# One table of keys in place of a planner: the order of all engines in a two-layer graph attention kernel

## The chip, the cores and the metric

The kernel runs on one core of a Trainium2 chip. The metric is the device time of one execution in microseconds; the median of the runs is compared. The core has five instruction streams that matter here: TensorE (PE in the profile, with its weight loads as PEld), VectorE (DVE), ScalarE (ACT), GpSimd (POOL) and SyncE (SP), which here only starts transfers. [...]

## The reference

The input is a batch of 128 graphs of 128 nodes with 512 features, and a 128x128 adjacency matrix with weights for each graph. Two layers of attention with 8 heads of 64 follow each other; everything is float32. Cut to what matters:

```
# layer 0
Q, K, V = x @ W_q + b_q, x @ W_k + b_k, x @ W_v + b_v        # split into 8 heads
scores  = Q K^T / 8 + a_i + c_j + b_g + log(adj + 1e-9)      # a = x @ w_g[:512], c = x @ w_g[512:]
x       = softmax(scores) V + x
# layer 1
q, k, v = x @ Wq.T + bq, x @ Wk.T + bk, x @ Wv.T + bv
logits  = q k^T / 8 + log(clip(adj, 1e-8))
out     = (softmax(logits) v) @ Wo.T + bo
result  = layer_norm(x + out) * gamma + beta
```

## The kernel before

**Tiling.** The graphs are taken in groups of four (`G = 4`), so each layer has 32 groups (`NG`), and the loop of `fast_path` runs over t = 0 to 63: layer 0 for t < 32, layer 1 from t = 32. A group is 512 rows of x, held transposed in `XT[t]`. Every projection is a 512x512 by 512x512 product, done by Strassen's scheme with seven products P1 to P7. Five of them (P1 to P5) are split once more by the same scheme (`inner`: seven pairs of matmuls 128 columns wide), and P6 and P7 are plain (`product`: four pairs of 256 columns each). Every matmul is issued as two halves of 64 rows of the stationary operand. In groups 0 and 32 all seven are plain. The sums of inputs that Strassen needs are made on POOL (`outer_sums`, `inner_sums`, buffers `T`, `innerB`, `innerT`, `inner3`); sums of products are made by ACT copies and DVE additions in and out of four PSUM banks `bankA` (two of them), `bankB` and `bankC` (`matrix`, buffers `t1`, `u2`, `u3`, `s5`). Layer 0 has three such matrices per group (v, q, k), layer 1 four (v, q, k and the output matrix of the group before, `o_matrix`).

**Attention.** `score` does the 32 pairs of small matmuls of two graphs into the PSUM tiles `s_0` and `s_1`, then for each graph one exp on ACT, and one DVE product with the adjacency, the result of which is called E in the code and `h` or `xT` in the profile (it lies in those buffers). So no logarithm is taken and the softmax is not shifted by its largest value. `mix` multiplies E by V with a column of ones for the sums; DVE divides. If a sum leaves a safe range, a slower general path, which is not part of this case, would be taken. In layer 0 the gates `a` and `c` of a graph come from two POOL products with rows of `w_g` and two ACT activations that add up along the row (`gates`, buffer `gw`, eight pairs per group); exp needs `c`. Results of layer 0 are written to DRAM twice, in natural order (`x1d_n`) and in 32x32 blocks (`x1d_b`), which layer 1 loads transposed. In layer 1 the mixed rows go through DRAM as blocks (`x1d_o`) and come back into `gw`, as input of the output matrix; the layer-1 input is added by an accumulating transfer on POOL's queue (`residual`), and ACT, DVE and POOL do the layer norm (`norm_and_store`).

**Order of the work.** The code above issues nothing. The class `Plan` stands in for the engines: `record` notes each instruction with the ones that it must follow (`preds`, from what they read and write), and TensorE work is noted in units (`unit`), with a place in the nominal order and a cost. `mark` notes where each group t begins. At the end `issue` emits all noted instructions in one sequence, and each engine gets its own in that order, so every instruction of the profile has the line L585. The sequence is made by `schedule`: a list scheduler with costs for each kind of instruction (`cost`, `wait`, `run`), forward and backward by turns, with random stirring; the best turn by its own reckoning is taken. Then `periodic` replaces the keys of the middle groups by a table: `PATTERNS` has one row for groups 1 to 31 and one for groups 34 to 62, each with a period and a key for every instruction of a group, so that every group there has the same order relative to the group before. The rest (groups 0, 32, 33, 63 and what follows) keeps the order of the list scheduler, and `refine` then goes through the whole sequence twice and moves single instructions where TensorE would wait by its reckoning.

**Change of layers.** In group 32 the four weights of layer 1 are loaded and combined on POOL (`combine_outer`, `combine_inner`, buffers `w` and `wi`), while the gates and mixes of group 31 and the first layer-1 products also need POOL, DVE and PE. **The end** is written out after the loop: the last group's output is done graph by graph with plain matmuls, and the layer norms of groups 62 and 63 are spread over DVE, ACT and POOL, each followed by its store.

Of the kernel before, what the change touches and what calls it, by code (L numbers as in the profile page):

```python
# [13 lines left out]
ALU = mybir.AluOpType  # L14
# [29 lines left out]
class Strassen:  # L44
# [45 lines left out]
    def inner_weight(t, x, i):  # L90
# [10 lines left out]

PATTERNS = (
    (1, 31, 42.01, [int(v) for v in '''
        413 877 68 1327 2833 345 136 0 481 1462 1395 1039 549 2070 3356 809 626 694 1573 2772 8615 4503 9355 9402
        10016 10549 6965 8662 3435 3628 3876 4166 2912 3559 5020 4772 4414 5116 5731 6384 4000 4731 5185 5690 8495
        8668 8247 9001 8812 9064 9081 9671 10254 10385 9751 9898 10465 10663 10006 10137 10742 4665 4713 4779 4921
        5005 5071 5142 5225 5273 5318 5448 5514 5557 5645 5750 4975 5055 5121 5148 5186 5252 5295 5378 5426 5471
        5964 6095 6204 6248 6523 5612 5708 5774 5801 6008 6074 6139 6258 6299 6343 6430 6504 6570 6604 6685 6751
        6860 6956 7013 7142 7213 6621 6816 6882 6909 6947 7121 7268 7352 7399 7501 6548 6663 6682 6781 8688 6321
        6672 6772 6889 7958 9627 9517 10863 9873 9172 7034 7674 8061 7269 7382 8476 8659 8950 9298 9432 7596 7777  # L110
        8279 9364 10130 10643 10753 10261 10371 10596 9875 13411 13500 6357 6414 6520 6587 6641 6707 6772 6868 6991
        7035 7081 7312 7356 7465 7509 7575 7638 6398 6461 6649 6676 6728 6847 6903 7100 7246 7291 7733 7777 7886
        7930 8008 8053 7370 7421 7488 7514 7552 7623 7689 7755 7820 7865 7980 8061 8127 8154 8192 8258 8301 8367
        8432 8477 8598 8099 8148 8215 8241 8389 8455 8613 8679 8753 8798 7611 7842 7908 7935 7973 8040 8105 8180
        8279 8324 8370 8569 8657 8775 8819 8898 8944 7952 8017 8171 8198 8236 8302 8345 8411 8454 8538 9014 9057
        9123 9167 9414 9460 8641 8710 8776 8803 8863 8929 8970 9036 9101 9145 9232 9304 9370 9397 9435 9501 9544
        9610 9697 9742 9812 9505 9588 9654 9734 9807 9934 10257 10323 10388 10484 9957 10448 10609 10210 10344
    '''.split()]),
    (34, 62, 52.97, [int(v) for v in '''
        756 2204 2814 0 1409 1736 47 3975 4224 5312 4734 3324 4472 4995 5064 5133 5243 5984 5482 3282 3934 5441 5202  # L120
        4181 4329 4420 4001 4228 4247 4712 4869 4492 4602 4537 4954 5120 4771 4898 5585 5728 5871 5077 5432 5519
        6320 6100 5943 6210 13343 12372 16647 4432 4493 4559 4872 5033 5099 5345 5411 5563 5608 5678 5722 5831 5875
        5953 4588 4858 4937 5055 5213 5388 5476 5646 5765 5810 6093 6181 6268 6378 6444 5897 5962 6028 6055 6137
        6203 6334 6400 6465 6509 5925 6006 6072 6099 6225 6291 6421 6487 6531 6575 6646 6503 6552 6619 6646 6815
        6891 6946 7012 7077 7121 5658 5787 5854 5880 5918 5985 6050 6116 6312 6356 6402 6487 6596 6684 6727 6881
        6927 6582 6640 6746 6773 6858 6925 6990 7182 7252 7296 7099 7165 7208 7318 7471 7559 6718 6771 6837 6864
        6902 6968 7033 7100 7143 7203 7276 7361 7427 7454 7492 7571 7624 7690 7733 7785 7907 7652 7755 7821 7848
        7951 8029 8126 8193 8345 8389 7194 7274 7340 7367 7405 7480 7536 7602 7667 7712 7757 7820 7864 7908 7995
        8061 8107 7384 7449 7515 7542 7580 7646 7689 7755 7798 7846 8170 8258 8367 8454 8520 8566 7919 8039 8143
        8170 8214 8280 8411 8477 8542 8586 7979 8083 8226 8253 8301 8367 8498 8564 8605 8650 8720 8612 8671 8880  # L130
        8941 9058 9124 9189 9444 9572 9656 8802 9212 9325 9037 9150 5250 6137 6006 6701 8050 7967 8198 8327 7481
        8758 8129 8511 8888 8690 8998 9962 10155 10224 7316 8956 8456 9066 8462 8627 8693 8720 8758 8825 9014 9080
        9276 9465 9594 9637 9681 9725 9874 8659 8715 8897 8924 9145 9269 9435 9605 9768 9813 10046 10112 10199 10243
        10314 8795 9102 9168 9195 9233 9299 9391 9635 10090 10134 10207 10287 10414 10441 10554 10621 10686 10752
        10817 10965 11036 10387 10467 10533 10560 10598 10664 10729 10795 10839 10883 10961 12127 12252 12065 12243
        12272 12287 12304 12392 12414 12489 12654 12892 12967 13096 13227 11121 12654 12860 12716 13074 13244 13094
        13275 13794 14034 14405 15135 14120 14694 14942 15416
    '''.split()]),
)


class Plan:
# [5 lines left out]

    ENGINES = ("tensor", "vector", "scalar", "gpsimd", "sync")
    HOP, JUDGED, MARGINS = 0.06, 0.06, (0.05, 0.1, 0.15, 0.2)  # L150
    SAME = dict(tensor=0.0, vector=0.1, scalar=0.1, gpsimd=0.05, sync=0.0)
    DONE = dict(tensor=0.19, vector=0.085, scalar=0.085, gpsimd=0.04, sync=0.0)
    SEEN = dict(tensor=0.055, vector=0.035, scalar=0.035, gpsimd=0.09, sync=0.03)
    PATIENCE, PASSES, STIR = 40.0, 12, 0.6
    GRAIN, LATE, ROUGH, TRIALS = 32, 0.8, 0.8, 3
    AHEAD, STALL, SWEEPS, CALM = 400, 0.1, 2, 2.0

    class Op:
        __slots__ = ("i", "engine", "calls", "cost", "lag", "pos", "preds", "succs", "kb", "start", "ls")
# [8 lines left out]
    def __init__(self, tc):  # L168
        self.tc, self.nc = tc, tc.nc
        self.ops, self.seen, self.masks, self.open, self.log, self.marks = [], {}, {}, None, [], []  # L170
        self.patterns, self.fixed = (), 0
        for name in self.ENGINES:
            setattr(self, name, Plan.Engine(self, name))
# [4 lines left out]
    @contextmanager  # L178
    def unit(self, pos, cost):
        self.open = self.op("tensor", cost, pos=pos)  # L180
        yield
        self.open = None

    def op(self, engine, cost, lag=0.0, pos=None):
        o = Plan.Op()
        o.i, o.engine, o.calls, o.cost, o.lag, o.pos = len(self.ops), engine, [], cost, lag, pos
        o.preds, o.succs = set(), []
        self.ops.append(o)
        return o

    def record(self, engine, method, args, kw):
        aps = [(k, a) for k, a in list(enumerate(args)) + list(kw.items()) if hasattr(a, "tensor")]
        if engine == "tensor":
            o = self.open
        else:
            o = self.op(engine, *self.cost(engine, method, [a for _, a in aps], kw, args))
        o.calls.append((engine, method, args, kw))
        for k, a in aps:
            if k not in (0, "accum_out"):
                self.touch(o, a, False)  # L200
        for k, a in aps:
            if k in (0, "accum_out"):
                self.touch(o, a, True)

    @staticmethod
    def cost(engine, method, aps, kw, args):
        n = max(a.free_size() if callable(a.free_size) else a.free_size for a in aps)
        psum = any(a.space == PSUM for a in aps)
        if method == "dma_start":
            if engine == "gpsimd":  # L210
                return 1.6, 6.5
            kb = (aps[0].size() if callable(aps[0].size) else aps[0].size) * 4 / 1024
            return (1.1 if kb == 128 else 0.68) if len(aps[0].shape) == 4 else 0.47, 1.8 + kb / 150
        if engine == "scalar":
            return (0.06 + 0.00085 * n + (0.08 if "scale" in kw or "bias" in kw else 0.0) + (0.13 if "accum_out" in kw else 0.0),)
        if engine == "vector":
            if method in ("transpose", "bn_stats"):
                return (0.01 + 0.00118 * n,)
            if not psum and method in ("tensor_tensor", "tensor_scalar_mul") and n == 512:
                return (1.2,)  # L220
            return (0.08 + 0.00103 * n + (0.055 if method == "scalar_tensor_tensor" else 0.0),)
        if ALU.pow in args:
            return (0.68,)
        return (0.135 + 0.00216 * n,)
# [59 lines left out]
    def wait(self, p, o):  # L284

        if p.lag:
            return p.lag + self.HOP
        if p.engine == o.engine:
            return self.SAME[p.engine]
        return self.DONE[p.engine] + self.SEEN[o.engine]  # L290

    def run(self, edges, key):

        ops, start = self.ops, [0.0] * len(self.ops)
        free, left, when = dict.fromkeys(self.ENGINES, 0.0), [0] * len(ops), [0.0] * len(ops)
# [1113 lines left out]
```

## Time and profile before

| | |
|---|---|
| runs | 3132.68, 3135.54, 3135.10 us; median 3135.1 |
| profiled execution | 3135.12 us, span 3133.3 us, mean TensorE clock 0.995 |
| PE | busy 3079.3 us, 98% of the span |
| PE weight loads | 2667.8 us, 85% |
| DVE | 2262.5 us, 72% |
| POOL | 2233.0 us, 71% |
| ACT | 1796.7 us, 57% |
| DMA | mean 109 GB/s, 341.89 MB |
| PE in 400 to 800 us (layer 0) | busy 398.35 of 400 us |
| PE in 2000 to 2400 us (layer 1) | busy 398.53 of 400 us |
| PE in 0 to 80 us | busy 71.33 us |
| PE in 1300 to 1600 us | busy 284.88 us |
| PE in 3060 to 3134 us | busy 53.26 us |

The span is the time from the first to the last instruction of the core; the profiled execution's own time is 1.8 us longer. The profile's page gives totals, slices of the span, the chain of work that ended last and the costliest groups of instructions. The trace can be asked for single stretches (windows), for what an engine waited for (waits), and for single instructions in order of time (timeline); there, square brackets show how long the engine had been idle before the instruction, and what ended that. [...]

### The profile page before, as it was taken

What the parts mean: (1) busy time and instruction counts of PE and PEld (TensorE: products, weight loads), DVE (VectorE), ACT (ScalarE), POOL (GpSimd) and SP (SyncE); (2) the same over time, 40 slices, a digit from 0 to 9 for tenths busy, and PEclk for the clock granted to TensorE, in tenths of its full rate; (3) what the DMA queues carried; (4) which work ended last, traced back from release to release, by engine and by line L of the source; (5) the groups of instructions that cost most, each with busy time, mean ns of one, the idle gap of its engine ahead of it and who ended that gap; (6) DMA issues with size and microseconds to landing.
All of it is one profiled execution on the core that took longest, in us unless ns stands there. A gap on an engine that the chain in (4) does not pass through costs nothing.

```text
span 3133.3 us, 121185 instructions
## 1 busy us (share of the span) xinstructions
PE 3079.3 (98%) x50394; PEld 2667.8 (85%) x50394; DVE 2262.5 (72%) x5075; ACT 1796.7 (57%) x5179; POOL 2233.0 (71%) x2713
## 2 busy tenths in 40 slices
PE   8999999999999999989999999999999999999997
PEld 6888888888888888867888888888888888888885
DVE  5677777777677767765677777777777777777776
ACT  2666666666666665644565655565655555555653
POOL 8766666676666676688677786868686868686775
PEclk9999999999999999999999999999999999999999
DMA  5555555555555555553444444443435353535343
GB/s 116 115 106 115 108 112 123 117 108 113 110 110 122 123 110 108 123 140 76 107 102 111 105 106 110 102 114 93 118 91 123 89 127 84 129 83 130 86 110 92
DMA packets 963100, 341.89 MB, mean 109 GB/s; under 512 B 864240, under 2 KB 871408, under 8 KB 962544
## 3 DMA queue, kind: packets, MB, share of 16 engines
q1 hardware_dynamic: 944272, 299.48, 40.7%
q0 software_dynamic: 16864, 32.51, 6.3%
q8 instruction: 397, 6.50, 0.8%
q10 hardware_dynamic: 1408, 2.10, 0.2%
q14 instruction: 159, 1.30, 0.1%
HBM read 192.42 MB, written 141.56 MB: 107 GB/s over the span
## 4 chain that ended last, share of the span: by engine, by line
PE 88%; POOL 4%; DVE 2%; ACT 2%; issue 2%; DMA 1%; SPq 0%; ACTq 0%; DVEq 0%; POOLq 0%
PE bankA L585 42%; PE bankB L585 16%; PE bankC L585 15%; PE s L585 15%; POOL gw L585 2%; ACT s L585 1%; DVE kT L585 1%; POOL w L585 1%; ACT gw L585 1%; DMA xT<-in_x_dram 1%; POOL T L585 1%; POOL wi L585 0%; SPq L585 0%; DVE bankB L585 0%; POOL inner L585 0%
## 5 line engine op out<-in xcount | busy, mean ns | idle before, releaser
L585 PE MATMUL bankA<-T,w 128*64 128x256 f32 (+1 forms) x4232 | 519.8, 351 | 1.1 <-ACT bankA L585 0.8
L585 DVE TENSOR_TENSOR bankA<-bankA,s 128x128 f32<-128x128 f32 x868 | 256.0, 295 | 209.1 <-PE bankA L585 178.5
L585 DVE TENSOR_TENSOR bankB<-bankB,s 128x128 f32<-128x128 f32 x650 | 193.0, 297 | 214.3 <-PE bankB L585 170.8
L585 PEld LDWEIGHTS bankA<-T,w 128*64 128x64 f32 x4232 | 276.3, 137 | 46.3 <-ACT bankA L585 1.0
L585 DVE TENSOR_TENSOR bankC<-bankC,s 128x128 f32<-128x128 f32 x652 | 192.4, 295 | 156.5 <-PE bankC L585 125.7
L585 ACT ACTIVATE bankA<-ident 128x256 f32<-128x256 f32 x434 | 167.5, 386 | 197.4 <-DVE kT L585 117.9
L585 PE MATMUL bankA<-w,T 128*64 128x256 f32 (+1 forms) x2116 | 271.2, 352 | 0.9 <-POOL w L585 0.9
L585 PE MATMUL s<-qT,kT 64*128 64x128 f32 x4096 | 263.1, 278 | 1.1 <-DVE kT L585 1.0
L585 ACT COPY s<-bankA 128x128 f32<-128x128 f32 x434 | 114.2, 263 | 258.1 <-PE bankA L585 253.6
L585 POOL TENSOR_TENSOR rs<-rs,minus_half 128x2 f32<-128x2 f32 (+1 forms) x66 | 47.6, 722 | 298.7 <-ACT rs L585 298.7
L585 PEld LDWEIGHTS s<-qT,kT 64*128 64x128 f32 x4096 | 238.6, 188 | 23.7 <-issue 19.1
L585 PE MATMUL bankC<-xT,w 128*64 128x128 f32 (+1 forms) x2296 | 228.2, 277 | 0.4 <-ACT bankC L585 0.4
L585 ACT ACTIVATE gw<-gw 128x512 f32<-128x512 f32 x256 | 159.7, 625 | 99.6 <-POOL gw L585 99.6
L585 POOL TENSOR_TENSOR gw<-xn,gw 128x512 f32<-128x512 f32 x128 | 163.3, 1277 | 55.6 <-ACT gw L585 48.3
L585 POOL TENSOR_TENSOR gw<-w,gw 128x512 f32<-128x512 f32 x128 | 164.9, 1290 | 48.2 <-ACT gw L585 46.2
L585 POOL TENSOR_TENSOR h<-h,gamma 128x512 f32<-128x512 f32 x121 | 154.7, 1280 | 36.7 <-ACT h L585 36.7
L585 POOL TENSOR_TENSOR innerB<-xT 128x256 f32<-128x256 f32 x62 | 45.8, 738 | 187.5 <-PE bankB L585 122.8
L585 ACT ACTIVATE bankC<-ident 128x256 f32<-128x256 f32 x326 | 126.7, 389 | 91.3 <-DVE kT L585 48.6
L585 DVE STREAM_TRANSPOSE xT<-xT 128x512 f32<-128x512 f32 x252 | 172.6, 695 | 8.4 <-DMA w<-in_x_dram 8.4
L585 ACT ACTIVATE bankB<-ident 128x256 f32<-128x256 f32 x325 | 124.3, 383 | 87.6 <-DVE qT L585 34.8
L585 POOL TENSOR_TENSOR T<-xT 128x512 f32<-128x512 f32 x96 | 122.9, 1280 | 66.6 <-DVE xT L585 66.5
L585 PE MATMUL bankA<-w,xn 128*64 128x256 f32 x1364 | 165.8, 352 | 0.1
(268 smaller groups left out, 10172.8 us busy)
## 6 DMA issues: line engine op xcount, KB each, us to landing
xT<-x1d_b SPq DMA_DIRECT2D x64, 512.0 KB, 6.0
xT<-in_x_dram SPq DMA_DIRECT2D x496, 64.0 KB, 3.2
x1d_o<-o SPq DMA_DIRECT2D x248, 128.0 KB, 4.7
gw<-x1d_o SPq DMA_DIRECT2D x62, 512.0 KB, 3.4
h<-x1d_n POOLq DMA_DIRECT2D x62, 512.0 KB, 6.9
out_dram<-h SPq DMA_DIRECT2D x60, 512.0 KB, 4.0
xn<-in_x_dram SPq DMA_DIRECT2D x32, 512.0 KB, 4.1
x1d_n<-w SPq DMA_DIRECT2D x32, 512.0 KB, 3.8
```

The lines of the kernel that those rows point to most:

```text
L585: self.tc.keep_in_program_order(getattr(getattr(self.nc, engine), method)(*args, **kw))
```

## The change

The planner inside `Plan` goes: `cost`, `wait`, `run`, `edges`, `retime`, `first_keys`, `advance`, `refine`, `periodic` and `schedule` are removed, with their constants. In their place `tabled` gives every instruction a key from a table, and the sequence is again made by taking, of the instructions whose predecessors have been taken, the one with the least key. `PATTERNS` has new keys for the middle groups (3 to 29 and 36 to 60, with a first start and a period each), and the new `REST` has a key for each instruction of what lies before, between and behind: `FIRST` (860 keys: the set-up and groups 0 to 2), `CHANGE` (1978 keys: groups 30 to 35) and `LAST` (1158 keys: groups 61 to 63 and the end). The keys are in hundredths. The cost that `mix` hands to `unit` is changed as well; `unit` no longer uses it. The recording of the instructions and the finding of predecessors stay, and so does everything in `fast_path` but that cost and the last two lines.

```diff
 PATTERNS = (
-    (1, 31, 42.01, [int(v) for v in '''
-        413 877 68 1327 2833 345 136 0 481 1462 1395 1039 549 2070 3356 809 626 694 1573 2772 8615 4503 9355 9402
...
+    (3, 29, 71.95, 41.905, [int(v) for v in '''
+        0 2091 1819 2159 3282 230 115 1491 1245 2355 2023 2457 1887 2274 3842 1559 2389 1423 1955 3593 6418 4033
...
-    (34, 62, 52.97, [int(v) for v in '''
-        756 2204 2814 0 1409 1736 47 3975 4224 5312 4734 3324 4472 4995 5064 5133 5243 5984 5482 3282 3934 5441 5202
...
+    (36, 60, 1503.84, 52.968, [int(v) for v in '''
+        0 1486 1548 492 2912 3531 445 3872 4580 5040 4709 3569 3679 4902 5164 5274 5526 5347 5868 4374 5233 5416
...
+FIRST = 0.00, [int(v) for v in '''
+        1538 7625 29872 1229 1777 0 0 47 47 141 141 188 94 94 914 470 517 0 410 484 510 584 460 534 560 645 423 235
...
+CHANGE = 18.03, [int(v) for v in '''
+        120210 118718 118536 119847 122871 119055 120492 118652 120764 121818 120877 120560 120278 119848 122129
...
+LAST = 2828.05, [int(v) for v in '''
+        0 765 957 47 2973 3592 4706 4539 4540 4968 4661 2591 3085 4830 4785 4831 5458 5519 6565 4829 5457 4969 5588
...
+REST = FIRST, CHANGE, LAST
...
-    def periodic(self, start):
...
-    def schedule(self):
...
+    def tabled(self):
+
+        ops, marks, key = self.ops, self.marks, []
+        for group in range(len(marks) + 1):
+            row = next((v for v in self.patterns if v[0] <= group - 1 <= v[1]), None)
+            if row is not None:
+                first, _, start, period, at = row
+                key += [start + period * (group - 1 - first) + v / 100 for v in at]
+            elif not group or any(v[1] == group - 2 for v in self.patterns):
+                start, at = self.rest[sum(v[1] < group for v in self.patterns)]
+                key += [start + v / 100 for v in at]
+        assert len(key) == len(ops)
         after, left = [[] for _ in ops], [len(o.preds) for o in ops]
         for o in ops:
             for q in o.preds:
                 after[q].append(o.i)
...
+        heap, turn = [(key[o.i], o.i) for o in ops if not o.preds], []
+        heapify(heap)
         while heap:
             i = heappop(heap)[1]
-            seq.append(i)
+            turn.append(ops[i])
             for j in after[i]:
                 left[j] -= 1
                 if not left[j]:
                     heappush(heap, (key[j], j))
-        return seq
...
+        return turn
 
     def issue(self):
-        for o in self.schedule():
+        for o in self.tabled():
             for engine, method, args, kw in o.calls:
...
-        with nc.unit(pos, 0.93):
+        with nc.unit(pos, 0.985):
...
-    nc.patterns = PATTERNS
+    nc.patterns, nc.rest = PATTERNS, REST
     nc.issue()
```

## The prediction

> **What bounds the kernel now.** I read the totals and the slices first, then the chain, then the windows by stage, then the waits and short pieces of the timeline. The totals:
>
> ```profile
> PE 3079.3 (98%) x50394; PEld 2667.8 (85%) x50394; DVE 2262.5 (72%) x5075; ACT 1796.7 (57%) x5179; POOL 2233.0 (71%) x2713
> PE 88%; POOL 4%; DVE 2%; ACT 2%; issue 2%; DMA 1%; SPq 0%; ACTq 0%; DVEq 0%; POOLq 0%
> ```
>
> TensorE (PE) sets the end: busy 98% of the span and 88% of the chain that ended last. So only time in which PE waits, or in which nothing runs on it, can be won. By busy time that is 3133.3 - 3079.3 = 54 us. The windows (from:to, length, busy us and count of PE, its weight loads, DVE, ACT, POOL, then clock, DMA share, GB/s) say where:
>
> ```profile
> 0.00:80.00 80.00, 71.33 (x820) 52.78 (x822) 46.17 (x75) 25.02 (x65) 63.95 (x110) 0.96 0.54 114
> 400.00:800.00 400.00, 398.35 (x6670) 345.12 (x6670) 286.28 (x652) 247.29 (x731) 260.00 (x287) 1.00 0.55 115
> 1300.00:1600.00 300.00, 284.88 (x4447) 237.62 (x4442) 197.35 (x429) 148.85 (x416) 230.13 (x312) 0.99 0.43 107
> 2000.00:2400.00 400.00, 398.53 (x6638) 352.78 (x6634) 302.44 (x684) 232.22 (x657) 304.81 (x376) 1.00 0.42 102
> 3060.00:3134.00 74.00, 53.26 (x662) 38.84 (x656) 44.89 (x94) 25.15 (x71) 38.16 (x47) 0.89 0.31 87
> ```
>
> The middle of either layer shows 1.5 us idle in 400; start, change of layers and end show 8.7, 15.1 and 20.7. But busy time hides short waits. In the trace consecutive pairs of half matmuls start 218 ns apart (128 columns), 432 ns (256 columns), 116.5 ns (mix) or 112 ns (score) when nothing waits; a pair whose wait clears late is merely recorded as longer (0.44 us for 4 in place of 0.39 below). So I summed start-to-start times. One matrix is 5x7 pairs at 0.218 plus 8 at 0.432 = 11.09 us. A group of layer 0 has three matrices, two scores (4.18) and four mixes (3.73): 41.2 us. Layer 1 has a fourth matrix: 52.3. The chain gives the measured group, from one piece and the same piece 27 groups later (start, length, what):
>
> ```profile
> 158.24 1.99 PE s L585 x32
> 1306.49 1.99 PE s L585 x32
> 1580.06 2.16 PE bankA L585 x24
> 3011.78 2.16 PE bankA L585 x24
> ```
>
> (1306.49-158.24)/27 = 42.53 and (3011.78-1580.06)/27 = 53.03 us: 1.3 us of waiting per group in layer 0, 0.7 in layer 1. By the same sums the excess over unstalled matmuls is 12.1 us in 0-80, 2.4 in 80-150, 42 in 150-1300, 28.5 in 1300-1600, 25 in 1600-3000 and 6 after it up to the last matmul (3114.4), with 18.9 us behind that matmul. Some 5.5 us in each middle are inside the scores and no order removes them.
>
> [...]
>
> **The change part by part.** Comparing the two kernels' issue orders, every engine issues the same number of instructions (25360 PE, 5130 DVE, 4957 ACT, 2725 POOL, 1581 SP by that count); nothing but order differs, and the waits that follow from it. Nothing is saved by work removed; the mix's changed unit cost is not read any more. All gains are waits.
>
> *Layer 1, middle (36-60).* The repeated wait is this one:
>
> ```profile
> 1640.06 0.39 PE L585 MATMUL bankC<-inner,w 128*64 128x128 f32 x4
> 1640.28 0.30 DVE L585 TENSOR_TENSOR bankB<-bankB,s 128x128 f32<-128x128 f32 x1 [0.57 <-PE bankB L585]
> 1640.63 0.44 PE L585 MATMUL bankB<-innerT,w 128*64 128x128 f32 x4 [0.18 <-DVE bankB L585]
> ```
>
> Between the matmul that releases bankB to DVE and bankB's next use PE has one pair (0.218) to do, and the 0.30 operation with its signals takes longer. About 0.35 us are lost per group. In the new order no DVE-released bank has under about 297 ns of slack by my sum (before -77), and places with at most 450 ns fall from 16 to 6 per two groups. I take 0.35 x 25 groups = 8.8 us. Below: 0.15, if the freed slack is used up by another wait (3.8); above 0.5 (12.5).
>
> *Layer 0, middle (3-29).* Per group waits of at least 120 ns sum to 0.60 us, short ones (mostly 30-50 ns) to 0.74. The largest, 378 ns in alternate groups, is a short DVE operation behind an E product that waits for exp on ACT, itself behind a gate activation:
>
> ```profile
> 232.15 0.63 ACT L585 ACTIVATE gw<-gw 128x512 f32<-128x512 f32 x1 [1.50 <-POOL gw L585]
> 232.91 1.09 ACT L585 ACTIVATE s<-s,c 128x1024 f32<-128x1024 f32 x1
> 234.03 1.22 DVE L585 SCALAR_TENSOR_TENSOR h<-adjT,s 128x1024 f32<-128x1024 f32 x1 [0.23 <-ACT s L585]
> 235.16 0.29 DVE L585 TENSOR_TENSOR bankC<-bankC,s 128x128 f32<-128x128 f32 x1
> 235.60 0.44 PE L585 MATMUL bankC<-w,inner 128*64 128x128 f32 x4 [0.21 <-DVE bankC L585]
> ```
>
> The new order puts exp ahead of the gate activations and the short PSUM operations ahead of or apart from E products. But one place per group has 142 ns of slack in both orders, and the small waits have no visible cure. I take two thirds of 0.60, so 0.4 x 27 = 10.8 us (0.1 to 0.6: 2.7 to 16). Moved back in exchange are the gates: their POOL products (1.28 us) have POOL at 65% here, so they are covered. Each DMA still has 10 us or more from its slot to its reader against 3-7 us landing (before 8.7): hidden; uncovered it would cost up to 5 us a group.
>
> *Change of layers.* PE's two longest waits:
>
> ```profile
> 1384.07 2.00 PE L585 MATMUL s<-v,h 128*64 128x65 f32 x32 [4.50 <-DVE h L585]
> 1388.08 2.00 PE L585 MATMUL s<-v,h 128*64 128x65 f32 x32 [2.01 <-DVE h L585]
> ```
>
> Two mixes stand some 0.7 us of PE work behind their own score, and exp waits for gates that POOL does between weight combines. In the new order they stand 12-23 us of PE work later with layer-1 value products between. That removes 4.5 + 2.0 = 6.5. A steady 300 us would carry about 6 of the 28.5 us excess, so 22 are special to this stretch. Of the other 15.5 (waits of 0.5-1.2 us on POOL weights and xT, on DVE, on ACT) I take two fifths, 6.5. Together 13. What is late next: POOL combines for WV, just in time in the new order, at most 1 us by POOL's sum. Range 8 to 18.
>
> *Start.* SP now issues graph 0's x first, not five transposed blocks of group 1. The 4.00 us wait of the first transposes on that x should fall by about half (DMA is saturated for the first 30 us either way). Gates are spread, so that the copies on ACT no longer stand behind eight of them (a 2.7 us wait on u at 37.4). 2 + 2.7 + 0.8 of small waits = 5.5. Against it: W_q's last quarter has about 5 MB queued ahead (4.15 before) and is wanted 1.8 us of PE work earlier; at 0.2 MB/us that could cost 0.85/0.2 + 1.8 = 6, leaving -0.5. Range -2 to 9.
>
> *End.* 24 DVE operations (13.5 us) stand behind the last product now; about 12 (5.5) in the new order: group 62's statistics are moved ahead. I take 5.5 of the 8, since the output's last store (5.3 us from the last DVE operation to the span's end) stays and a residual DMA may hold PE 1.5 us. Range 3 to 8.
>
> Sum: 8.8 + 10.8 + 13 + 5.5 + 5.5 = 43.6 us. The profiled execution took 3135.12 (span 3133.3, 1.8 around it), the median of the runs shown is 3135.1: the same. 3135.1 - 43.6 = 3091.5; I say 3092.
>
> **The rivals.** *Less:* the middles keep their short waits, and each removed stall shows up at the next tight place; 4 us from layer 1, 3 from layer 0, 8 at the change, 2 and 3 at the ends: 20 us, 3115. For it: 0.74 of layer 0's 1.3 us are waits of 30-50 ns that I can't tie to an order. Against: the -77 ns place in layer 1 is really gone. *More:* all waits of 120 ns or longer go, middles 0.60 x 27 + 0.5 x 25 = 29, change 18, ends 7 + 8: 62 us, 3073. *Nothing, because PE is full:* the 54 us idle are mostly start and end, and the order only shifts them: 3135. Against: the 6.5 us at 1384 are plain. *Slower:* a queue-blocking wait once in every period, such as one POOL sum or one DMA landing late behind its new neighbour on an in-order queue. The ends and change give about 24, so it decides from 24/52 = 0.46 us per period if the middles gain nothing else; one late landing of 1 us over 52 groups ends at 3135 - 24 + 52 = 3163. Against: my slack sum shows no such place, but its durations are of one order only.
>
> **How the numbers follow.** About 0.2% (6 us) is what a measurement here can tell from no change. Chances: forecast (3082 to 3101) 0.56; less (3101 to 3127) 0.22; more (3070 to 3082) 0.14; same 0.04; slower 0.04. Faster 0.92. Range 3077 to 3118: it leaves out most of "more" (0.09) and the last two with the tail of "less" (0.11).
>
> **What would show it.** Right: the chain's group near 42.1 in layer 0 and 52.7 in layer 1; no layer-1 line of PE bankB waiting on DVE bankB once per group; no mix waiting above 1 us at the change; some 25 us from the last product's stretch to the end in place of 31. Wrong: groups still at 42.5 or 53.0, a wait on a weight DMA in the first 40 us, or a new wait with a count near 27 in the list of PE's waits.

## The result

| | median us | range us | ratio to before |
|---|---|---|---|
| before | 3135.1 | 3132.7 to 3135.5 | |
| changed kernel | 3107.5 | 3104.8 to 3111.5 | 0.9914 (0.9897 to 0.9932) |

The changed kernel is 27.7 us faster; the forecast was 43 us (3092), with a range of 3077 to 3118. The time falls in the band that the prediction called *less* (3101 to 3127), and the 7 us between the fastest and the slowest run of the changed kernel are more than the kernel before shows (3). The totals of the changed kernel are again those of a kernel that TensorE fills:

```profile
PE 3061.0 (98%) x50394; PEld 2665.0 (86%) x50394; DVE 2290.9 (74%) x5075; ACT 1803.5 (58%) x5179; POOL 2240.3 (72%) x2713
```

The windows by stage (from:to, length, busy us and count of PE, its weight loads, DVE, ACT, POOL, then clock, DMA share, GB/s), to be held against those of before:

```profile
0.00:80.00 80.00, 71.45 (x874) 54.78 (x876) 46.53 (x79) 28.37 (x75) 67.85 (x111) 1.00 0.49 114
400.00:800.00 400.00, 399.47 (x6762) 349.15 (x6758) 295.21 (x663) 254.01 (x747) 267.80 (x292) 1.00 0.55 114
1300.00:1600.00 300.00, 291.96 (x4636) 249.07 (x4634) 212.02 (x446) 154.51 (x433) 239.30 (x326) 0.99 0.47 114
2000.00:2400.00 400.00, 397.45 (x6610) 351.41 (x6607) 304.75 (x683) 229.86 (x653) 292.24 (x362) 1.00 0.48 111
```

The count in brackets says more than the busy time. In the same 80, 400 and 300 us PE now gets through 874 matmuls (before 820), 6762 (6670) and 4636 (4447). In 2000 to 2400, the middle of layer 1, it is 6610, where the kernel before did 6638: there the new order is slower. The chain says the same per group, from one score and the same score 26 groups later in layer 0, and 23 groups later in layer 1:

```profile
153.21 1.99 PE s L526 x32
1245.55 1.99 PE s L526 x32
1674.82 1.99 PE s L526 x32
2901.10 1.99 PE s L526 x32
```

(1245.55 - 153.21)/26 = 42.01 us, before 42.53. (2901.10 - 1674.82)/23 = 53.32 us, before 53.03. The sums of start-to-start times over unstalled matmuls, made as in the prediction, give by stage ("excess" is the time beyond what the same matmuls take when nothing waits):

| stage | excess before | after | gain | forecast |
|---|---|---|---|---|
| 0 to 150 | 14.5 | 10.2 | 4.3 | 5.5 |
| 150 to 1300 (layer 0) | 42.3 | 29.5 | 12.8 | 10.8 |
| 1300 to 1600 (change of layers) | 28.5 | 15.2 | 13.3 | 13 |
| 1600 to 3000 (layer 1) | 25.2 | 34.0 | -8.9 | 8.8 |
| from 3000 | | | 3.9, the rest of the 25.4 us between the two spans | 5.5 |

So nearly all of the missing 18 us are in layer 1 (17.7), while the errors of the other stages cancel. And in layer 1 it is not that the gain stayed out: the sign is wrong. PE's waits (what for, us in total, times, longest) show what is new; the first line is of the kernel before, the others of the changed one:

```profile
PE bankB L585 <- DVE bankB L585: 6.0, 31, 0.5
PE bankC L526 <- DVE good_sum L526: 8.6, 1, 8.6
PE bankA L526 <- DVE bankA L526: 8.6, 13, 1.6
PE bankB L526 <- issue: 5.5, 1, 5.5
PE bankB L526 <- DVE bankB L526: 3.5, 2, 2.3
PE bankC L526 <- POOL xT L526: 3.0, 1, 3.0
```

The wait of `bankB` for DVE, 31 times 0.2 us before, has gone from the middle of layer 1, and so have the 4.5 and 2.0 us of the mixes at the change. In their place stand 13 waits of up to 1.6 us for a sum of DVE in `bankA`, all but a few in layer 1; one wait of 5.5 us at the change that the profile can't name; 3.0 us at the start; and 8.6 us before PE's very last matmul, behind the last product. Each of these was followed up. The two waits of `bankB` for DVE that are left, 1.1 us at 1283 and 2.3 us at 3044, were not.

**Where the wait in layer 1 comes from.** DVE's own waits hold a line that the kernel before does not have:

```profile
DVE gw L526 <- DMA gw<-x1d_o: 15.9, 18, 2.9
```

The mixed rows of layer 1 go to DRAM in two halves, each by four stores of `o` and one load into `gw`, and DVE turns what came back. In the group at 1790, SyncE's queue (start, length, what) ran like this:

```profile
1793.09 1.29 SPq L526 DMA_DIRECT2D x1d_o<-o  x2
1794.43 0.95 SPq L526 DMA_DIRECT2D adjT<-x1d_a  x1
1795.42 0.51 SPq L526 DMA_DIRECT2D xT<-x1d_b  x1
1795.96 1.28 SPq L526 DMA_DIRECT2D x1d_o<-o  x2
1806.36 0.33 SPq L526 DMA_DIRECT2D gw<-x1d_o  x1
```

Between the first two stores of the second half and the last two, the new order sets the adjacency (256 KB) and half of xT (512 KB) of the next group but one. POOL's queue issued one of its accumulating loads (512 KB) at 1795.46, just ahead of the last two stores, and a second at 1804.04. The last two stores took 9.7 us to land, the load of `gw` could only be issued then, at 1806.36, and landed at 1812.43. DVE's turning of it had been next in its queue since 1811.1, and a sum in `bankA` that PE needed stood behind:

```profile
1812.45 1.30 DVE L526 STREAM_TRANSPOSE gw<-gw 128x512 f32<-128x512 f32 x2 [1.36 <-DMA gw<-x1d_o]
1813.68 0.27 DVE L526 TENSOR_TENSOR bankA<-bankA,s 128x128 f32<-128x128 f32 x1
1814.00 0.44 PE L526 MATMUL bankA<-xT,wi 128*64 128x128 f32 x4 [1.10 <-DVE bankA L526]
```

1.36 us of DVE waiting became 1.10 us of PE waiting. Over the middle of layer 1 the medians from the issue of a second half's first store, in us, are:

| | last store landed | gw landed (longest) | its load took | DVE turns it |
|---|---|---|---|---|
| before | 11.7 | 15.1 (16.3) | 3.3 | 20.3 |
| changed | 12.4 | 18.2 (19.8) | 5.6 | 18.2 |

The new order allows this path 2 us less and makes it 3 us longer. (DVE's 18.2 in the changed kernel has its own waiting in it; where it hardly waits, in the experiment `l1_bulk_late`, it turns the rows at 17.7.) What was left of the 5 us is nothing, so a transfer that is disturbed goes through to PE. In the kernel before the groups in the middle of layer 1 take 53.0 us almost without exception; here they take between 52.8 and 54.7. That may be why the runs of the changed kernel lie further apart, but no run shows it.

**The 5.5 us at the change.** The chain of the profile doesn't name it, but DVE's and POOL's timelines do. A DVE instruction of 0.60 us in the kernel before (the first half of the product of `bv` with the output weights) takes 6.30 us, the value copy that PE needs stands behind it, and it ends when POOL's unbroken run of operations ends. The first line gives the shortest, middle and longest time in ns of the two halves in the kernel before, the others are of the changed kernel:

```profile
L585 DVE TENSOR_SCALAR gw<-w,bv x2: 541/570/599, 1389.5 to 1391.8; 128x256 f32<-128x256 f32 x2
1370.06 6.30 DVE L526 TENSOR_SCALAR gw<-w,bv 128x256 f32<-128x256 f32 x1
1376.28 0.68 DVE L526 TENSOR_TENSOR v<-bankB,u 128x512 f32<-128x512 f32 x1
1372.51 3.71 POOL L526 TENSOR_TENSOR w<-w 128x512 f32<-128x512 f32 x3
1376.28 0.29 POOL L526 TENSOR_SCALAR ok<-rc 128x32 f32<-128x32 f32 x1
```

The instruction lasted through seven POOL operations one after the other, from 1370.05 to 1376.22, and ended 0.15 us behind the last of them. Its second half, which started in a gap of POOL's, took 0.31 us. In the kernel before, the first half ended 0.15 us behind the end of a POOL operation too; of its 0.60 us some 0.3 may be waiting, an estimate from the 0.31 of the undisturbed half. That POOL's run held the DVE instruction is the author's reading of these times; by what means is not shown.

### The profile page after: what moved, and what is told of

Its sections match the earlier page's. It is cut to its first block, busy times and chain, and to the rows that moved or that the text cites. A ratio compares the mean times of both kernels' runs of the same rounds, so it can differ in the third digit from the quotient of the medians.

```text
span 3107.9 us, 121261 instructions
## 1 busy us (share of the span) xinstructions
PE 3061.0 (98%) x50394; PEld 2665.0 (86%) x50394; DVE 2290.9 (74%) x5075; ACT 1803.5 (58%) x5179; POOL 2240.3 (72%) x2713
## 3 DMA queue, kind: packets, MB, share of 16 engines
q14 instruction: 158, 1.29, 0.1%
## 4 chain that ended last, share of the span: by engine, by line
PE 74%; POOL 11%; DMA 8%; SPq 2%; issue 2%; DVE 2%; ACT 1%; ACTq 0%; POOLq 0%; DVEq 0%
PE bankA L526 36%; PE s L526 13%; PE bankB L526 13%; PE bankC L526 13%; DMA x1d_o<-o 4%; POOL h L526 3%; DMA gw<-x1d_o 3%; POOL T L526 2%; SPq L526 2%; POOL innerB L526 1%; POOL xn L526 1%; POOL innerT L526 1%; DVE gw L526 1%; ACT h L526 0%; POOL xT L526 0%
## 5 line engine op out<-in xcount | busy, mean ns | idle before, releaser
L526 PE MATMUL bankA<-T,w 128*64 128x256 f32 (+1 forms) x4232 | 541.0, 351 | 1.1 <-ACT bankA L526 1.1
L526 POOL TENSOR_TENSOR gw<-w,gw 128x512 f32<-128x512 f32 x128 | 163.5, 1283 | 155.3 <-ACT gw L526 110.2
L526 POOL TENSOR_TENSOR xn<-gw 128x512 f32<-128x512 f32 x62 | 79.3, 1279 | 137.2 <-PE bankA L526 131.9
L526 ACT ACTIVATE s<-s,c 128x1024 f32<-128x1024 f32 x128 | 139.7, 1092 | 55.2 <-PE s L526 55.2
L526 ACT COPY s<-bankB 128x128 f32<-128x128 f32 x325 | 86.4, 266 | 139.6 <-PE bankB L526 137.8
L526 PEld LDWEIGHTS bankC<-xT,w 128*64 128x64 f32 x2296 | 142.1, 137 | 25.3 <-ACT bankC L526 16.0
L526 POOL TENSOR_TENSOR innerB<-gw 128x256 f32<-128x256 f32 x31 | 22.5, 727 | 194.7 <-DVE gw L526 194.7
```

The lines of the kernel that those rows point to most:

```text
L526: self.tc.keep_in_program_order(getattr(getattr(self.nc, engine), method)(*args, **kw))
```

## The experiments

All are edits of the changed kernel (3107.5 us). Most add some lines to `tabled`, just behind the check on the number of keys, which change the keys of a few instructions (`marks[t] + n` is the n-th noted instruction of group t). Ratios are to the kernel before, which ran along each time.

**Layer 1: the two loads behind the gw load.**

```diff
+for t in range(36, 61):
+    key[marks[t] + 6] += 6.05  # adjT, from 2 us behind the first store of o to just behind gw's load
+    key[marks[t] + 3] += 5.68  # second half of xT, likewise
```

> The changed kernel, with two loads of groups 36 to 60 moved on SyncE's queue: the adjacency (256 KB) and the second half of xT (512 KB) stand behind the load of gw and no longer between the four stores of o. Theory A (the round trip of the mixed rows through DRAM is slowed by the loads that the new order put among its stores, DVE's queue is held at the turning of gw, and PE behind it): DVE's waits for the gw load fall from 15.9 us (18 times) to under 3, PE's waits of bankA for DVE bankA from 8.6 us to under 2, and the time from 3107.5 by some 9 to about 3098 (3094 to 3102). Rival B (the accumulating loads of h on POOL's queue slow the round trip, whatever stands on SyncE's): DVE's waits for gw stay above 10 us, the time within 3 us of 3107.5. Rival C (xT or the adjacency is late in the new place): a new wait of DVE or PE for xT, and a time above 3108.

Measured: 3092.0 us, ratio 0.987 (0.9854 to 0.9885). The waits, of DVE and of PE:

```profile
DVE gw L529 <- DMA gw<-x1d_o: 1.4, 1, 1.4
PE bankA L529 <- DVE bankA L529: 1.8, 3, 1.0
```

The last store of a second half now lands after 8.7 us and `gw` after 12.3, its load takes 3.4, and a group of layer 1 takes (2872.04 - 1658.59)/23 = 52.76 us by the same scores. Rival B as it was put falls, since POOL's accumulating loads stayed where they were and DVE's waits fell to 1.4 us; rival C falls too, since layer 1 shows no wait for xT. But the trace points to a share of POOL's loads in the delay. In this run the first three stores of a second half, issued before POOL's load, take 3.1 to 3.5 us in the median, and the fourth, issued just behind it with none of SyncE's loads among the stores, still takes 6.5 (in the changed kernel the last two take 8.8). And the load of `gw`, issued 3.7 us sooner, now starts ahead of POOL's second load and not behind it. Against the kernel before that is 0.27 us per group won, near the 0.35 that the prediction gave the bank's wait; against the changed kernel 0.56 x 25 = 14 us in layer 1 of this profile. The window at 1340 to 1410 shows PE busy 68.25 us here and 63.70 in the changed kernel: in the profiled run the `bv` instruction took 0.58 us and the 5.5 us wait did not come. That run is the fastest of the four (3086.8 us); the others took 3091.4 to 3094.1. Whether the wait came in those isn't known. If it stayed out of them too, some 5 of the 15.5 us in the median (14 by the ratios to the kernel before) are no work of these loads.

**Layer 1: the old order back in groups 36 to 60.** The order as a whole comes from a list here: the instructions of these groups stand as in the kernel before, all others as in the changed one, merged by the TensorE work ahead of each.

```diff
-        heap, turn = [(key[o.i], o.i) for o in ops if not o.preds], []
...
+        for d in steps:
+            i += d
+            turn.append(self.ops[i])
```

> The changed kernel, with the order of before for all engines in groups 36 to 60 alone; where the groups meet, instructions merge by the amount of TensorE work ahead of them. Theory A (the new order of layer 1 lost about 9 us against the old one there, though its PSUM wait is gone): 3107.5 - 9 = about 3098 (3094 to 3102), with the bankB wait of about 0.35 us per group back and no wait of DVE for gw. Rival D (the new layer-1 order gained the 8.8 us that were forecast, and the shortfall lies elsewhere): about 3116.

Measured: 3113.6 us, 0.9935 (0.9922 to 0.9949): slower than the changed kernel, against theory A's 3098, and near what rival D said. But in the middle a group takes (2902.43 - 1682.21)/23 = 53.05 us, with the `bankB` wait of 0.355 us back in every one and no wait of DVE for `gw`. That is the old order's pace, 0.27 us per group better than the new one's. The loss is at the two seams: nine waits of 0.4 to 1.8 us between 1565 and 1640 and seven of 0.4 to 2.5 us from 2896 to 2973, some 12 us, which neither kernel has. So the run's time settles nothing between A and D; its pace per group speaks for A. These two tables, each made to follow its own neighbours, couldn't be swapped singly without that loss.

**Layer 1: the turning behind the sum.** The loads stay, and the two turnings of gw's second half go behind the sum in `bankA` that they held up.

```diff
+for t in range(36, 61):
+    key[marks[t] + 249] = key[marks[t] + 181] + 0.001  # turning of gw's second half, behind the next sum in bankA
+    key[marks[t] + 250] = key[marks[t] + 181] + 0.002
```

> The changed kernel, with one change on DVE's queue in groups 36 to 60: the two turnings of gw's second half stand behind the next sum in bankA, and no longer in front of it; the loads stay as they are. Theory A (a late gw load stops PE because DVE's queue is held at the turning, with that sum behind it): gw is as late as before, PE's waits of bankA for DVE bankA fall from 8.6 us to under 3 us, and the time by 6 to 9 us, to about 3099. Rival I (PE would be stopped by the late gw itself, a little later, by way of POOL's sums): the wait turns up under POOL's buffers, and the time stays within 3 us of the changed kernel's.

Measured: 3128.4 us, 0.9978 (0.997 to 0.9986), 21 us slower. Neither theory said this. In DVE's timeline of one group:

```profile
2085.38 0.30 DVE L529 TENSOR_TENSOR bankA<-bankA,s 128x128 f32<-128x128 f32 x1 [1.06 <-PE bankA L529]
2085.59 1.29 DVE L529 STREAM_TRANSPOSE gw<-gw 128x512 f32<-128x512 f32 x2
2086.81 0.65 DVE L529 BATCH_NORM_STATS2 st<-h 128x6 f32<-128x512 f32 x1
2087.38 0.28 DVE L529 TENSOR_TENSOR bankA<-bankA,s 128x128 f32<-128x128 f32 x1
```

DVE has a gap of 1.06 us in front of that sum, and the turnings had filled it. Behind the sum they and one statistics operation (1.29 + 0.65 us) stand before the next sum in `bankA`, which PE then waits 0.44 us for in every group, and waits of 0.2 to 0.3 us for POOL's and ACT's work follow on it. `gw` landed as late as in the changed kernel (18.3 us in the median), but DVE came to the turnings only at 19.3 and so waited for it 1.9 us in all, 4 times. The run thus takes the wait for `gw` away and puts another in its place; how much the first was worth it can't say. What it shows is that this other place on DVE's queue is worse for 1.3 us of work, though DVE is busy 74% of the span.

**Change of layers: the bv instruction moved, and done by ScalarE.** Two kernels on the same wait.

```diff
+key[marks[32] + 33] = key[marks[32] + 32] - 0.001  # first half of weigh_rows(0), next to its second half
```

> The changed kernel, with one DVE instruction of group 32 moved: the first half of the product of bv with the output weights (0.57 us before, 6.30 us in the changed kernel) stands next to its second half, some 4 us of TensorE work later. Theory E ([...] the value copy behind it was late, and PE waited 5.7 us at 1377): that wait of PE falls to under 1 us, the time by 5 to about 3102.5. Rival F (the operands of that PE work came late anyway, from POOL or from a load): a wait of at least 4 us stays there, and the time is within 2 us of 3107.5.

Measured: 3100.0 us, 0.9894 (0.9879 to 0.9909). The instruction and its second half together take 2.13 us, and PE's 5.5 us wait is gone (busy 68.44 us in 1340 to 1410). The 7.5 us against the changed kernel are more than the wait; by the ratios to the kernel before they are some 6.

```diff
-                nc.vector.tensor_scalar(o, w, b, None, ALU.mult)
+                nc.scalar.activation(o, w, AF.Identity, scale=b)
```

> The changed kernel, with the first two products of bv with the output weights done by ScalarE in place of DVE, at the same places of the order. Theory E ([...] nothing else was late): the 6.3 us instruction is gone, the 5.5 us wait of PE at 1377 too, and the time falls by 5 to 6 us against the changed kernel, to about 3102. Rival F (PE's work there would come late anyway): a wait of 4 us or more stays at that place, and the time is within 2 us of 3107.5.

Measured: 3099.9 us, 0.9892 (0.9876 to 0.9909), PE busy 68.25 us in that window, no wait of more than 1.0 us of it there. (The profiled run was the slowest of the four, 3111.7 us, with 21.0 us of DVE's waits for `gw`; the others took 3098.2 to 3100.7.) Nothing but the engine of two instructions differs, and the wait goes with the DVE instruction: rival F falls. How long that instruction takes is a matter of chance: in seven profiles with the same order at that place it took 6.3 us in six (changed kernel, its repetition, and the experiments `undo_l1`, `good_early`, `l0_gate_ahead` and `l1_turn_behind`), and 0.58 us in the seventh (`l1_bulk_late`). Its start doesn't tell the two apart: 14 to 48 ns behind the start of the same POOL operation in five of the six, 36 ns in the seventh. In all six it ended 0.15 us behind the end of POOL's run, and in the seventh 0.15 us behind the end of one POOL operation inside that run. So it was this instruction's 6.3 us that PE waited for; that POOL's run held it remains the author's estimate, from the two ending 0.15 us apart.

**The end: the good counts early.**

```diff
+end = marks[64]
+key[end + 86], key[end + 106], key[end + 111] = 3058.10, 3058.75, 3059.40  # good_sum, its matmul, bad
```

> The changed kernel, with the last three small instructions of the end (the sum over the good counts, its matmul, and the comparison that gives bad) moved from behind the last DVE operation to some 6 us ahead of it, behind the last POOL count, as in the kernel before. Theory G (what follows the kernel's body waits for bad, about 6.4 us from it to the end of the span, where the last store needs only about 2.3 us behind its landing): the stretch from the last DVE operation to the end shrinks, and the time falls by 2 to 2.5 us to about 3105. Rival H (the last store sets the end either way): no change beyond 0.5 us.

`good_sum` adds up the flags of sums in the safe range, and `bad` decides whether the general path is taken. In the changed kernel they stand behind all else on DVE:

```profile
3100.92 0.21 DVE L526 TENSOR_REDUCE good_sum<-good 128x1 f32<-128x64 f32 x1
3101.41 0.14 DVE L526 TENSOR_SCALAR bad<-bankC 1x1 int32<-1x1 f32 x1 [0.28 <-PE bankC L526]
```

The last store lands at 3103.10, and the span ends at 3107.9, 4.8 us later and 6.3 us behind `bad`. With the counts early, `bad` is done at 3088.93, the last store lands at 3098.06, and the span ends at 3100.3, 2.2 us behind it (before: 2.3 us). That is 2.5 us less behind the last store. But the store itself lands later: it takes 3.7 us in place of 2.1 and lands 12.3 us behind the last product in place of 10.5. From the last product to the end the stretch falls from 15.3 to 14.5 us only. So neither G's 2 to 2.5 us nor H's at most 0.5 came, but 0.8; why the store is slower with the counts early was not tested. The times, 3103.9 us and 0.9908 (0.9893 to 0.9923), can't tell 0.8 us from nothing.

**Layer 0: one gate ahead of exp again.**

```diff
+for t in range(3, 30):
+    key[marks[t] + 57] = key[marks[t] + 289] - 0.01  # a gate's activation, ahead of the exp of the last graph
```

> The changed kernel, with one ScalarE instruction of groups 3 to 29 moved back to where the kernel before had it: a gate activation (0.63 us and 0.2 us for the sum) stands ahead of the exp of a group's last graph. Theory J (exp ahead of the gates was the cure of the 378 ns wait in alternate groups): 0.2 to 0.38 us per group come back, 27 groups, so 5 to 10 us slower than the changed kernel, and a group of layer 0 of about 42.3 us. Rival K (the gain in layer 0 came from the places of the short PSUM sums, and exp has slack enough): within 2 us of the changed kernel, a group of 42.0 us.

Measured: 3116.1 us, 0.9941 (0.9928 to 0.9955), 8.4 us slower than the changed kernel's repetition. By scores 25 groups apart a group takes:

```profile
182.80 1.99 PE s L528 x32
1241.35 1.99 PE s L528 x32
```

(1241.35 - 182.80)/25 = 42.34 us, where the changed kernel has 42.01. In the new order this one instruction of 0.8 us is worth 0.33 us per group, of the 0.52 gained in all. Theory J stands.

**The changed kernel once more.**

> The changed kernel itself, for comparison beside the runs of the same chip: within 3 us of 3107.5, with DVE's waits for the gw load between 10 and 17 us, and the 6.3 us DVE instruction of group 32 there or not[...] (it was 0.6 us in one of the kernels with the same order there).

Measured: 3107.7 us (3105.9 to 3113.8), 0.991 (0.9895 to 0.9926); DVE's waits for gw 18.1 us, 21 times; the `bv` instruction 6.29 us. The profiled execution is one of the longer ones in both sets, so its gw waits are probably above the middle.

**Three edits together** (the loads, the `bv` instruction, the good counts, as above).

> The changed kernel with three edits together: the two layer-1 loads behind the gw load, the bv instruction moved, the good counts early. If the three act apart from each other (10 us from the loads, 5.7 us from the PE wait in group 32, which the first of them had been spared by chance, 2.3 us at the end): 3106 - 18 = about 3088 (3085 to 3091). If they overlap, it stays at 3092.

Measured: 3089.8 us, 0.9854 (0.9839 to 0.9869), 1.8 us above the expected middle and inside its range. A layer-1 group takes 52.82 us.

**The start.** Two tries, each on top of the three edits, at the 3.0 us that PE waits for a sum inside xT. The first moved six sums behind the wrong instruction (the sum that PE waits for is an earlier one of 256 columns):

```diff
+for n, r in enumerate((213, 143, 156, 140, 199, 207)):  # sums of group 0's weights, behind a sum of group 1's xT
+    key[marks[0] + r] = key[marks[1] + 42] + 0.01 * (n + 1)
```

> The kernel with three edits, and one more at the start: six of POOL's sums for the layer-0 weights (0.45 to 0.53 us each, 2.8 us in all), which TensorE needs 10 us later or more, stand behind the sum of group 1's xT that PE waits 3.0 us for at 50. If POOL's queue is what makes that sum late, the wait falls to under 0.5 us and the time from 3089.8 to about 3087. If the sum is late by its own operands, or a weight sum is then late in turn, it stays within 1 us of 3089.8.

Measured: 3088.1 us, 0.9854 (0.9838 to 0.9871), and the wait still 3.0 us: no effect, as it must be. The second took the right one:

```diff
+for n, r in enumerate((88, 157, 90, 148, 197)):  # sums of group 0's weights, behind the first sum in group 1's xT
+    key[marks[0] + r] = key[marks[1] + 34] + 0.01 * (n + 1)
```

> The kernel with three edits, and a fourth at the start in place of the one that moved the wrong sums: five of POOL's operations on the layer-0 weights (2.6 us in all in the trace, wanted by TensorE some 10 us later) stand behind the first sum inside group 1's xT (256 columns), which was the one that PE waits 3.0 us for near 50. If POOL's queue makes it late: the wait falls to about 0.5 us and the ratio to the kernel before from 0.9854 to about 0.9846, some 2.5 us. If the sum is held by its own operands, the wait stays at 3 us.

Measured: 3088.0 us, 0.9852 (0.9836 to 0.9869). The wait fell from 3.0 to 0.7 us, so POOL's queue made most of it; but waits of 0.4, 0.5 and 0.3 us for POOL's `T`, `innerT` and `wi` came in the 20 us behind it. POOL is busy 69 of the first 80 us, and what is put back there is late in turn. Nothing that these times can tell was won.

Both this version and the one with three edits beat both kernels: 3088 us, 1.5% below the kernel before, where the changed kernel is 0.9% below.

## Why the prediction was right, and where not

The time lies inside the range, 15.5 us above the forecast. That it does is in part luck: layer 1 alone missed by 17.7 us, far below the 3.8 us that were its lower case, and the misses of the other stages cancel.

- **What bounds the kernel, and where the time lies.** Right. But for the stretch behind the last product, all that was won or lost are waits of PE, in the stages named. Busy time alone could not have shown layer 0's gain: idle time there fell from 1.65 to 0.53 us per 400, the groups by 0.52 us of 42.53.
- **Layer 0, 10.8 us.** Right, somewhat low: 12.8. The named cause, exp behind a gate on ACT, carries most of it (0.33 of 0.52 us per group).
- **Change of layers, 13 us.** The sum is right (13.3), but by two errors that cancel. The two mixes' waits went as forecast. "What is late next" was given as at most 1 us on POOL's weight sums; it was 5.5 us, by way of a DVE instruction that had cost 0.60 us and now took 6.30, to the end of a run of POOL's. The other waits there then gave some 12 us, in place of the 6.5 allowed for.
- **Start, 5.5 us.** Somewhat high: 4.3. The wait for x went; the feared wait for W_q's last quarter was 0.7 us or less. POOL's run near 50 took 3.0 of the gain. The 0.2 MB/us of the prediction stand in the windows of the first 30 us (217 GB/s in both kernels); "saturated either way" holds for the kernel before alone, with a DMA share of 1.02 there and of 0.84 in the changed kernel.
- **End, 5.5 us.** High: 3.9, in the range of 3 to 8. The last product is followed by 15.3 us in place of 18.9. The steps that failed are two. DVE's rest behind the last product was put at 5.5 us, and it takes 9.0 (15 operations, before 26 in 13.6 us). And the end of the span was put 5.3 us behind the last DVE operation in either order, and it is 6.3 now, with `bad` last; of this, putting the counts early won 0.8.
- **Layer 1, 8.8 us.** Wrong in sign: -8.9. The forecast mechanism is right: the 0.35 us wait for `bankB` is gone, and with the loads moved a group takes 0.27 us less than before. The step that failed is that transfers were put at nothing: "Each DMA still has 10 us or more from its slot to its reader against 3-7 us landing (before 8.7): hidden". That stands under layer 0, and the paragraph on layer 1 says nothing more of transfers. The last stores of a second half took 8.8 us in the median. And the load of `gw` doesn't start at its place in the order; it waits on SyncE for the stores (9.0 us in the group at 1790), so two transfers in a row lie in the path. DVE was ready for the result about 17.7 us from the first store (as `l1_bulk_late` shows); the path took 18.2 in the median and 19.8 at the longest.
- **The rivals.** "Slower" named the mechanism, one DMA landing late behind its new neighbour on an in-order queue, and 0.46 us per period as the point from which it would decide. It came, in layer 1 alone, at about 0.56 us per group there, with the start, the change and layer 0 to outweigh it. "Less" was right in its band (3101 to 3127) and wrong in its reason: it wasn't short waits that stayed.

What stays open: how far the waits of gw in the median run are those of the profiled one; how the delay of the stores divides between SyncE's and POOL's loads; what part of the 15.5 us of `l1_bulk_late` is the chance at the `bv` instruction; and what held that instruction.

## What to carry to other kernels

A new order moves transfers too: add up a path through DRAM as a chain, with the landing of the stores before the issue of the load, and hold it against the time from the first issue to the reader, not each transfer against its own slot. Here, bulk loads that nobody was waiting for did better behind the load of such a round trip than among its stores (3092.0 us against 3107.5). When an instruction in the trace takes ten times its usual time, look at what the other engines were doing: here the 6.30 us in place of 0.60 ended with seven POOL operations in a row. And when a wait goes, follow its stretch to the end: at the end of this kernel 2.5 us won behind the last store were mostly lost again in the store.

## What the runs showed of the hardware

- DVE kept to the order of its queue. In the changed kernel the sum in `bankA` that stood behind the two turnings started at 1813.68, though the last writes to `bankA` had ended at 1812.03 (TensorE) and 1812.90 (ScalarE), and the last to an `s` at 1813.10. With the keys exchanged (`l1_turn_behind`) the sum ran first, at 2085.38, and the turnings at 2085.59.
- A DVE instruction (128x256, a product with a column) took 6.3 us in place of 0.60 while POOL ran seven operations without a gap, and was done within 0.15 us of POOL's first pause. It was so in six of seven profiles with that order; in the seventh, and in the kernel before, with POOL at work too, it took 0.6 us. An instruction of the same form that started in a gap of POOL's took 0.31 us. With the same products on ScalarE PE had no such wait.
- In one group, stores of 128 KB took 3.1 us when issued ahead of 768 KB of loads on the same queue, and 9.7 us behind them, with a 512 KB accumulating load on POOL's queue at the same time. With the 768 KB moved away, a store just behind POOL's load took 6.5 us in the median, and those ahead of it 3.1 to 3.5.
- From the last small DVE result that the kernel's branch depends on to the end of the span were 6.3 us in the changed kernel; from the landing of the last store 2.2 to 2.3 us, when that result was early. The last store itself took 2.1 us with the result late, and 3.7 with it early.
